# A scan's product for four channel groups in one instruction, the experts' second product by halves, and a new order of the work, in a six-layer transformer and state-space kernel

## The chip, the cores and the metric

The kernel runs on one core of a Trainium2 chip. The metric is the device time in microseconds (us). The core has five engines that run side by side, each with its own queue of instructions: TensorE (PE in the profile; PEld is its loading of weights), VectorE (DVE), ScalarE (ACT), GpSimd (POOL) and SyncE (SP), which issues nearly all transfers here. An engine takes its instructions strictly in the order of its queue, so one that waits holds up all behind it. SBUF is the on-chip memory of 128 partitions; PSUM holds TensorE's results, in 8 banks of 128x512 float32.

## The reference

Four rows of 512 tokens with 128 features go through six residual layers, each on a layer norm of `x`:

```python
x = x + 0.5 * tree(ln(x))      # T: three routed trees give q, k, v; then one attention
x = x + attention(ln(x))       # h: 16 heads, rope, slopes
x = x + 0.5 * tree(ln(x))      # t
x = x + 0.5 * experts(ln(x))   # e: 8 experts, top 2, and a shared one
x = x + mamba(ln(x))           # s: state-space scan
x = x + 0.5 * experts(ln(x))   # f
```

An expert is `(silu(x @ w1.T) * (x @ w3.T)) @ w2.T`, here computed for all 8 and weighted with the routing weight (zero for those not taken), and a ninth, shared expert without a weight. The state-space layer has 256 channels with 16 states each:

```python
def step(h, inp):
    x_t, dt_t, B_t, C_t = inp
    dA = jnp.exp(dt_t[..., None] * A)
    h = dA * h + (dt_t * x_t)[..., None] * B_t[:, None, :]
    y = jnp.einsum('bdn,bn->bd', h, C_t)
    return (h, y)
```

## The kernel before

**Layout.** Features or channels lie on partitions and the 512 tokens of a row along the free axis. Each of the four rows is a chain of its own through the six layers, and layers of different rows run side by side. The names T0 to T3, h0 to h3, t0, e0, s0, f0 and so on are layer and row. A row's layer can start when the same row's layer before it is done.

**The scan (`state_main`).** A tile of 128 partitions holds 32 channels times 4 states. For each half `c` of the channels (2) there are four channel groups `g` of 32 and four state groups `q` of 4, so 32 tiles of 128x512 in each row, 128 in all. For one of them: TensorE spreads B over the partitions into PSUM (`state_b`, once for each `q`, L976); ScalarE makes the decay, `exp(dt * A)`, into a PSUM bank (L988); DVE multiplies `state_b` with `dtxs` (dt times x, L989) and runs the scan over the tokens in place (L990); GpSimd multiplies with C (`cs`, L991). When the four groups of a `q` are through, TensorE adds up their states (`sums`, L941). `dts` and `dtxs` come by transfers that read a row of channels from DRAM four times over (`spread`), 256 KB each: one of each for every `g`, eight for a half.

**The experts (`expert_main`).** For expert `e` and half `c`, TensorE makes two first products of three matmuls each in a rounded float32 format (helper `mm3`, L173 to L175; a number is split into a high and a low part), ScalarE a tanh (L765), DVE two products (L766, L772; in one case of nine GpSimd does the second one). This gives `u0` and `u1`. `second` multiplies both with `w2` into one PSUM bank: 8 matmuls of 128x128 in float32, 4 token tiles `i` times 2 halves `c`, which run as 16 passes (L780). For the 8 routed experts ScalarE scales the result (L790) and GpSimd adds it to `x` (L791); for the shared one, the last, DVE scales and adds in one (L793). When the last layer of a row is done, `store` writes it in one transfer of 256 KB (L1013).

**What sets the order.** Three things. `TIMES` gives each layer of each row a start and an end in arbitrary units for its preparation and its main part; the steps of all jobs are recorded in the order of these times. Inside a job, later steps are put off by a count of steps (`LAG` for trees, `LAG_MIX` for attention, `LAG_EXPERT`, `LAG_STATE`), so that, for instance, `sums` of a `q` are recorded five scan steps after its last group. The framework's own scheduler then moves instructions of one engine past each other and assigns addresses; the numbers in `BUFS` limit how many buffers of a kind are in use at once, and `BANKS` the same for PSUM. So a change of times or buffers changes the order on every engine, that of the transfers in SyncE's queue too.

Of the kernel before, what the change touches and what calls it, by code (L numbers as in the profile page):

```python
# [21 lines left out]
ALU = mybir.AluOpType  # L22
AX = mybir.AxisListType

P = 128
# [13 lines left out]


TIMES = dict(
    loads=(-189.8, -159.8),
    split=(19.6, 79.6),
    T0=(-58.8, -46.7, -14.1, 23.0, 12.7, 34.3),
    T1=(-1.4, 10.7, 26.1, 58.8, 60.4, 75.2),
    T2=(117.2, 127.5, 80.3, 138.4, 137.5, 160.7),
    T3=(97.6, 109.7, 125.5, 214.9, 203.8, 239.4),
    h0=(18.3, 35.0, 46.6, 115.7),
    h1=(85.2, 102.6, 114.5, 205.2),
    h2=(176.0, 193.3, 208.5, 282.9),  # L50
    h3=(241.0, 257.7, 278.8, 374.3),
    t0=(194.1, 204.5, 200.8, 246.1, 245.5, 261.8),
    t1=(326.8, 331.0, 355.5, 422.5, 467.1, 493.7),
    t2=(389.1, 402.4, 396.2, 454.3, 452.2, 490.1),
    t3=(466.1, 478.2, 486.9, 527.6, 531.1, 552.6),
    e0=(283.2, 284.2, 274.8, 345.6),
    e1=(397.8, 412.1, 420.6, 483.0),
    e2=(493.7, 507.9, 514.9, 572.4),
    e3=(570.5, 584.7, 588.8, 639.0),
    consts=(473.4, 474.4),  # L60
    s0=(360.4, 403.4, 402.0, 488.0),
    s1=(470.9, 515.1, 513.4, 595.5),
    s2=(570.4, 613.4, 617.5, 703.4),
    s3=(638.4, 681.3, 690.0, 776.9),
    f0=(572.6, 586.8, 621.9, 690.9),
    f1=(645.2, 659.4, 665.3, 729.5),
    f2=(702.6, 716.8, 728.6, 797.0),
    f3=(798.5, 810.1, 787.3, 878.5),
)
HEAD_LAG = 0.39  # L70

# [34 lines left out]

# [6 lines left out]
def macaron(ctx: ExitStack, tc: tile.TileContext, t: dict, stages: int = 6):  # L113
# [641 lines left out]
    def expert_main(b, st, last):  # L755
        xn = st.xn
        weights = [fetch_expert(e) for e in range(AHEAD)]

        def first(e, c):
            w13 = [weights[e][0][:, k, :] for k in range(2)]  # L760
            ps1, ps3 = bank("moe_1"), bank("moe_3")
            mm3(ps1, [m[:, ts(c, P)] for m in w13], xn)
            mm3(ps3, [m[:, ts(2 + c, P)] for m in w13], xn)
            u = work(f"u{c}")
            nc.scalar.activation(u, ps1, AF.Tanh, scale=0.5)  # L765
            nc.vector.scalar_tensor_tensor(u, u, 1.0, ps1, ALU.add, ALU.mult)  # L766
            if (2 * e + c) % POOL_E[0] < POOL_E[1]:
                v = work("v3")
                nc.scalar.copy(v, ps3)
                nc.gpsimd.tensor_mul(u, u, v)  # L770
            else:
                nc.vector.tensor_mul(u, u, ps3)  # L772
            return u

        def second(e, h):
            w2 = weights[e - e % 4][1]
            acc = bank("moe_acc")
            for i in range(NT):
                for c in range(2):
                    nc.tensor.matmul(  # L780
                        acc[:, ts(i, P)],
                        lhsT=h[c][:, ts(i, P)],
                        rhs=w2[:, e % 4 * 2 + c, :],
                        start=(c == 0),
                        stop=(c == 1),
                    )
            if e < EXPERTS:
                y = work("y")
                for i in range(NT):
                    nc.scalar.mul(y[:, ts(i, P)], acc[:, ts(i, P)], st.comb[:, i, e : e + 1])  # L790
                nc.gpsimd.tensor_add(flat(x[b]), flat(x[b]), y)  # L791
            else:
                nc.vector.scalar_tensor_tensor(  # L793
                    flat(x[b]), acc, 0.25, flat(x[b]), ALU.mult, ALU.add
                )
# [136 lines left out]
    def state_main(b, st, consts):  # L932
# [4 lines left out]
        def sums(c, q, hs, last):  # L937
            if q == 0:
                accs[c] = bank("state_acc")
            for g in range(4):  # L940
                mm = nc.tensor.matmul(  # L941
                    accs[c][32 * g : 32 * g + 32, :],
                    lhsT=gather,
                    rhs=hs[g],
                    start=(q == 0),
                    stop=(q == GROUPS - 1),
                )
# [16 lines left out]

        later = Later(LAG_STATE)
        for c in range(2):
            dt, dtx = [], []
            rows = t["state_rows"][b, c].rearrange("m (g r) s -> m g r s", r=CH)
            for g in range(4):
                for m, (name, to) in enumerate((("dts", dt), ("dtxs", dtx))):  # L970
                    to.append(work(name))
                    spread(to[g], rows[m, g])
            for q in range(GROUPS):

                bs = bank("state_b")
# [4 lines left out]
                    start=True,  # L980
                    stop=True,
                )
                hs = []
                for g in range(4):
                    k = (4 * c + g) * GROUPS + q
                    dA, h = bank("decay"), work("states")
                    hs.append(h)
                    nc.scalar.activation(dA, dt[g], AF.Exp, scale=A[:, k : k + 1])  # L988
                    nc.vector.tensor_mul(h, bs, dtx[g])  # L989
                    nc.vector.tensor_tensor_scan(h, dA, h, 0.0, ALU.mult, ALU.add)  # L990
                    last = nc.gpsimd.tensor_mul(h, h, cs[:, q])  # L991
                    later.step()
                    yield
# [356 lines left out]
```

## Time and profile before

| What | Value |
|---|---|
| time, median of 3 runs (lowest, highest) | 1130.23 us (1128.74, 1132.4) |
| the profiled execution's own time | 1134.71 us |
| its span, first to last instruction | 1132.9 us |
| granted clock of TensorE, mean | 0.983 |
| TensorE busy from 0 to 28 us | 10.96 us |
| TensorE, DVE busy from 300 to 600 us | 299.10, 223.88 us |
| TensorE, DVE busy from 600 to 1050 us | 409.47, 422.95 us |
| last matmuls of the layers s0, s1, s2, s3 | 683, 827, 988, 1074 us |
| first matmul of f3's experts | 1083 us |

In the profile's groups stand line, engine and operation, the tiles written and read with shape, the number of instructions, then the busy time in us and the mean duration of one in ns, then the idle time of the engine just before them and what ended it. In a table of windows the columns are, after the stretch and its length, busy time and number of instructions of PE, PEld, DVE, ACT and POOL, then the clock granted to TensorE (1.00 is full speed), the share of time that the transfer engines were busy, and GB/s. In a timeline: start, length, engine, line, operation, tiles and count; in brackets the idle time before it and what ended that.

### The profile page before, as it was taken

To read this page: it belongs to the slowest core of one execution; us is meant where nothing else is said; L and a number is where in the kernel's file an instruction comes from. 1 tells how busy PE (TensorE), PEld (TensorE's weight loads), DVE (VectorE), ACT (ScalarE), POOL (GpSimd) and SP (SyncE) were. 2 spreads that over 40 slices of the span, in tenths; PEclk is the share of its full clock that TensorE was granted. 3 is DMA by queue.
4 is the path that set the end of the run, shared out by engine and by line. 5 is a ranking of instruction groups with operands and counts; after the bars stand their busy time and mean duration, and the time that the engine had idled before them with its cause. 6 is when DMAs were issued, how large, how long until landed. Compare 5 with 4: busy or idle time off the path is not lost.

```text
span 1132.9 us, 16461 instructions
## 1 busy us (share of the span) xinstructions
PE 1065.0 (94%) x5536; PEld 717.4 (63%) x5536; DVE 903.5 (80%) x2151; ACT 516.4 (46%) x1078; POOL 408.3 (36%) x392
## 2 busy tenths in 40 slices
PE   3999999999999999999999999999598989997998
PEld 2666655566666767765566766567276646754787
DVE  4566886587576887775799997899989989999864
ACT  2231423332322555444443544465576557564544
POOL 2215231002100323220324651356626647666523
PEclk9999999999999999999999999999899989997999
DMA  7885845321542212243743334832137424742320
GB/s 217 261 254 168 284 109 119 84 69 57 123 124 93 65 37 69 87 112 115 208 137 139 117 94 107 277 130 107 38 117 254 133 66 146 249 121 70 113 88 10
DMA packets 79651, 146.41 MB, mean 129 GB/s; under 512 B 7536, under 2 KB 39664, under 8 KB 79568
## 3 DMA queue, kind: packets, MB, share of 16 engines
q1 hardware_dynamic: 79280, 145.07, 42.6%
q8 instruction: 44, 0.72, 0.3%
q14 instruction: 39, 0.32, 0.1%
q10 hardware_dynamic: 288, 0.30, 0.1%
HBM read 125.35 MB, written 13.70 MB: 123 GB/s over the span
## 4 chain that ended last, share of the span: by engine, by line
PE 61%; DVE 17%; issue 4%; ACT 4%; POOL 2%; DMA 1%; SPq 1%; POOLq 0%; ACTq 0%; DVEq 0%
PE tree_acc L410 9%; PE moe_acc L780 7%; DVE states L990 6%; PE head_acc L608 4%; PE head_sc L640 4%; PE moe L173 4%; PE head_max L564 4%; PE moe L175 3%; PE moe L174 3%; DVE states L989 3%; PE tree_mm L173 3%; PE tree_mm L175 3%; PE tree_mm L174 3%; PE state_acc L941 2%; DVE u L766 2%
## 5 line engine op out<-in xcount | busy, mean ns | idle before, releaser
L991 POOL TENSOR_TENSOR states<-states,cs 128x512 f32<-128x512 f32 x128 | 163.8, 1284 | 146.0 <-DVE states L990 87.8
L410 PE MATMUL tree_acc<-full,ring 128*128 128x512 f32 x384 | 193.4, 599 | 5.9 <-DVE full L400 4.9
L572 DVE CUSTOM_DVE_ANT_0 head_max<-head_max,kept 128x128 f32<-128x128 f32 (+3 forms) x256 | 126.8, 495 | 61.0 <-PE head_max L564 58.5
L400 DVE SCALAR_TENSOR_TENSOR full<-tree_mm,kept,mask 128x512 f32<-128x512 f32 x188 | 137.8, 746 | 42.4 <-PE tree_mm L175 37.7
L656 ACT ACTIVATE pt<-head_sc 128x512 f32<-128x512 f32 (+1 forms) x176 | 95.3, 559 | 139.2 <-PE head_sc L648 132.4
L780 PEld LDWEIGHTS moe_acc<-ring,u 128*128 128x128 f32 x1152 | 141.9, 195 | 21.2 <-DVE u L772 6.2
L990 DVE TENSOR_TENSOR_SCAN states<-decay,states 128x512 f32<-128x512 f32 x128 | 154.8, 1216 | 0.5 <-ACT decay L988 0.2
L780 PE MATMUL moe_acc<-ring,u 128*128 128x128 f32 x1152 | 146.4, 280 | 5.3 <-DVE u L772 3.1
L173 PE MATMUL moe<-xl,ring 128*128 128x512 f32 x288 | 129.1, 448 | 13.3 <-DVE u L766 4.7
L791 POOL TENSOR_TENSOR kept<-kept,y 128x512 f32<-128x512 f32 x64 | 83.0, 1298 | 142.2 <-ACT y L790 133.7
L988 ACT ACTIVATE decay<-dts,kept 128x512 f32<-128x512 f32 x128 | 88.5, 696 | 83.9 <-DVE states L990 67.0
L765 ACT ACTIVATE u<-moe 128x512 f32<-128x512 f32 x144 | 86.4, 601 | 72.2 <-PE moe L175 70.5
L174 PE MATMUL moe<-xh,ring 128*128 128x512 f32 x288 | 116.8, 405 | 0.0
L175 PE MATMUL moe<-xh,ring 128*128 128x512 f32 x288 | 115.7, 402 | 0.0
L766 DVE SCALAR_TENSOR_TENSOR u<-u,moe 128x512 f32<-128x512 f32 x144 | 97.4, 678 | 17.7 <-ACT u L765 15.2
L790 ACT ACTIVATE y<-moe_acc,scratch 128x128 f32<-128x128 f32 x256 | 73.3, 367 | 74.5 <-PE moe_acc L780 72.6
L548 POOL TENSOR_SCALAR km<-k_bias,kept 128x512 fp32r<-128x512 f32 x64 | 43.6, 699 | 157.2 <-PE head_sc L640 110.6
L173 PE MATMUL tree_mm<-xl,ring 128*128 128x512 f32 x188 | 98.1, 524 | 0.2 <-DVE states L990 0.2
L173 PEld LDWEIGHTS moe<-xl,ring 128*128 128x128 f32 x288 | 55.1, 191 | 63.5 <-DVE u L766 13.5
L410 PEld LDWEIGHTS tree_acc<-full,ring 128*128 128x128 f32 x384 | 70.8, 191 | 38.4 <-issue 19.9
L564 PE MATMUL head_max<-km,q_bias 120*128 120x512 f32 (+2 forms) x192 | 92.0, 479 | 1.1 <-ACT p L446 1.1
L989 DVE TENSOR_TENSOR states<-state_b,dtxs 128x512 f32<-128x512 f32 x128 | 85.9, 683 | 4.7 <-DMA dtxs<-state_rows 3.6
(257 smaller groups left out, 1946.1 us busy)
## 6 DMA issues: line engine op xcount, KB each, us to landing
ring<-moe_parts SPq DMA_DIRECT2D x72, 512.0 KB
ring<-tree_parts SPq DMA_DIRECT2D x42, 512.0 KB
ring<-in_fff_w SPq DMA_DIRECT2D x24, 512.0 KB
mask<-fff_taken SPq DMA_DIRECT2D x48, 256.0 KB
ring<-in_moe_w SPq DMA_DIRECT2D x16, 512.0 KB
dts<-state_rows SPq DMA_DIRECT2D x32, 256.0 KB
dtxs<-state_rows SPq DMA_DIRECT2D x32, 256.0 KB
moe_parts<-moe_w SPq DMA_DIRECT2D x9, 512.0 KB
```

The costliest lines, as they stand in the source:

```text
L173: nc.tensor.matmul(ps, lhsT=lh, rhs=rl, start=start, stop=False)
L174: nc.tensor.matmul(ps, lhsT=ll, rhs=rh, start=False, stop=False)
L175: nc.tensor.matmul(ps, lhsT=lh, rhs=rh, start=False, stop=stop)
L400: nc.vector.scalar_tensor_tensor(full, ps, neg_b1[:, n : n + 1], st.masks[k][:, c, :], ALU.max, ALU.mult)
L410: nc.tensor.matmul(acc, lhsT=weights[k][1][:, c, :], rhs=h, start=(c == 0), stop=False)
L564: nc.tensor.matmul(view, lhsT=qs[:R_MAX, g, ts(i, P)], rhs=km[j0 // 2][:R_MAX, j0 % 2 : j0 % 2 + each, :kw], start=True, stop=True,)
L572: nc.vector.tensor_tensor_reduce(view[:, n, :], view[:, n, :], future[:, S - kw :], -1.0, float(np.finfo(np.float32).max), ALU.add, ALU.mi ...
L766: nc.vector.scalar_tensor_tensor(u, u, 1.0, ps1, ALU.add, ALU.mult)
L780: nc.tensor.matmul(acc[:, ts(i, P)], lhsT=h[c][:, ts(i, P)], rhs=w2[:, e % 4 * 2 + c, :], start=(c == 0), stop=(c == 1),)
L989: nc.vector.tensor_mul(h, bs, dtx[g])
L990: nc.vector.tensor_tensor_scan(h, dA, h, 0.0, ALU.mult, ALU.add)
L991: last = nc.gpsimd.tensor_mul(h, h, cs[:, q])
```

## The change

It has five parts.

1. In the scan, one DVE product of 128x2048 takes the place of four of 128x512. `state_b` is read four times over. `states` becomes one tile for the four groups of a `q`, and `dtxs` one tile for the four groups of a half, filled by four transfers as before. The scans, GpSimd's products and the sums work on slices.
2. The experts' second product runs over the halves `c` outside and the token tiles `i` inside; only the first matmul of the bank starts it and only the last one closes it.
3. For the shared expert of the last layer of row 3, the order is by token tiles as before, DVE adds each 128x128 tile by itself, and each is stored at once by a transfer of 64 KB. The other rows are stored as before.
4. `TIMES` has new values for nearly all jobs, and LAG goes from 5 to 6, LAG_MIX from 4 to 3, LAG_STATE from 5 to 6.
5. The buffer counts change: `xl`, `v3`, `dt`, `pos` and `dts` have one fewer, `u1` and `xs` one more, `dtxs` goes from 6 tiles of 128x512 to 2 of 128x2048, and `states` from 8 of 128x512 to 8 of 128x2048. In the built programs the new `states` lie at three addresses and `dtxs` at two.

In the built programs the transfers of one half's `dts` and `dtxs`, which alternated, now go out with the four of `dtxs` together. At the start, the first tree's second weights (`fff_w2_0`) stand behind three of the small attention weights instead of one.

```diff
@@ TIMES (some of them)
-    loads=(-189.8, -159.8),
+    loads=(-149.2, -119.2),
-    T2=(117.2, 127.5, 80.3, 138.4, 137.5, 160.7),
+    T2=(94.5, 104.8, 73.9, 132.0, 128.3, 151.5),
-    h2=(176.0, 193.3, 208.5, 282.9),
-    h3=(241.0, 257.7, 278.8, 374.3),
+    h2=(171.0, 188.3, 208.5, 309.7),
+    h3=(247.4, 264.1, 297.6, 393.1),
...
-    f2=(702.6, 716.8, 728.6, 797.0),
-    f3=(798.5, 810.1, 787.3, 878.5),
+    f2=(684.0, 698.2, 722.7, 791.1),
+    f3=(845.7, 859.1, 830.7, 935.8),
@@
-LAG, LAG_MIX, LAG_EXPERT, LAG_STATE = 5, 4, 3, 5
+LAG, LAG_MIX, LAG_EXPERT, LAG_STATE = 6, 3, 3, 6
@@ BUFS (what changes of each line)
-    **dict(ring=7, stage=5, b1=1, b2=1, ln=3, xh=1, xl=4),
+    **dict(ring=7, stage=5, b1=1, b2=1, ln=3, xh=1, xl=3),
-    **dict(moe_w=1, lgT=1, u0=4, u1=2, y=2, v3=2),
-    **dict(hid=1, xs=2, sz=2, conv=1, xd=1, xb=2, cs=1, dt=2, dtx=2, pos=2, dts=7, dtxs=6, states=8),
+    **dict(moe_w=1, lgT=1, u0=4, u1=3, y=2, v3=1),
+    **dict(hid=1, xs=3, sz=2, conv=1, xd=1, xb=2, cs=1, dt=1, dtx=2, pos=1, dts=6, dtxs=2, states=8),
@@ expert_main, second
-            for i in range(NT):
-                for c in range(2):
-                    nc.tensor.matmul(
-                        acc[:, ts(i, P)],
-                        lhsT=h[c][:, ts(i, P)],
-                        rhs=w2[:, e % 4 * 2 + c, :],
-                        start=(c == 0),
-                        stop=(c == 1),
-                    )
+            at_end = last and b == B - 1 and e == EXPERTS
+            order = [(c, i) for c in range(2) for i in range(NT)]
+            for c, i in sorted(order, key=lambda ci: ci[::-1]) if at_end else order:
+                nc.tensor.matmul(
+                    acc[:, ts(i, P)],
+                    lhsT=h[c][:, ts(i, P)],
+                    rhs=w2[:, e % 4 * 2 + c, :],
+                    start=(c == 0 and (at_end or i == 0)),
+                    stop=(c == 1 and (at_end or i == NT - 1)),
+                )
...
-            else:
+            elif not at_end:
                 nc.vector.scalar_tensor_tensor(
                     flat(x[b]), acc, 0.25, flat(x[b]), ALU.mult, ALU.add
                 )
+            else:
+                for i in range(NT):
+                    out = x[b][:, i, :]
+                    nc.vector.scalar_tensor_tensor(out, acc[:, ts(i, P)], 0.25, out, ALU.mult, ALU.add)
+                    nc.sync.dma_start(out=t["out"][b, ts(i, P)], in_=out)
...
-        if last:
+        if last and b < B - 1:
             store(b)
@@ state_main
-                    rhs=hs[g],
+                    rhs=hs[:, g, :],
...
-            dt, dtx = [], []
+            dt, dtx = [], work("dtxs", (4, S))
             rows = t["state_rows"][b, c].rearrange("m (g r) s -> m g r s", r=CH)
             for g in range(4):
-                for m, (name, to) in enumerate((("dts", dt), ("dtxs", dtx))):
-                    to.append(work(name))
-                    spread(to[g], rows[m, g])
+                dt.append(work("dts"))
+                for m, to in enumerate((dt[g], dtx[:, g, :])):
+                    spread(to, rows[m, g])
...
-                hs = []
+                hs = work("states", (4, S))
+                nc.vector.tensor_mul(hs, dtx, bs.unsqueeze(1).to_broadcast([P, 4, S]))
                 for g in range(4):
                     k = (4 * c + g) * GROUPS + q
-                    dA, h = bank("decay"), work("states")
-                    hs.append(h)
+                    dA, h = bank("decay"), hs[:, g, :]
                     nc.scalar.activation(dA, dt[g], AF.Exp, scale=A[:, k : k + 1])
-                    nc.vector.tensor_mul(h, bs, dtx[g])
                     nc.vector.tensor_tensor_scan(h, dA, h, 0.0, ALU.mult, ALU.add)
```

More of the change, by code (lines that the diff above doesn't have):

```diff
@@ L41 @@
 TIMES = dict(
-    loads=(-189.8, -159.8),
-    split=(19.6, 79.6),
-    T0=(-58.8, -46.7, -14.1, 23.0, 12.7, 34.3),
+    loads=(-149.2, -119.2),
+    split=(20.2, 80.2),
+    T0=(-58.9, -46.8, -14.2, 22.9, 11.2, 32.8),
     T1=(-1.4, 10.7, 26.1, 58.8, 60.4, 75.2),
-    T2=(117.2, 127.5, 80.3, 138.4, 137.5, 160.7),
-    T3=(97.6, 109.7, 125.5, 214.9, 203.8, 239.4),
-    h0=(18.3, 35.0, 46.6, 115.7),
-    h1=(85.2, 102.6, 114.5, 205.2),
-    h2=(176.0, 193.3, 208.5, 282.9),
-    h3=(241.0, 257.7, 278.8, 374.3),
[L52 to L58, printed above, removed]
+    T2=(94.5, 104.8, 73.9, 132.0, 128.3, 151.5),
+    T3=(97.6, 109.7, 125.5, 214.9, 202.7, 238.3),
+    h0=(16.2, 32.9, 44.5, 113.6),
+    h1=(88.3, 105.7, 119.2, 209.5),
+    h2=(171.0, 188.3, 208.5, 309.7),
+    h3=(247.4, 264.1, 297.6, 393.1),
+    t0=(180.6, 191.0, 207.3, 252.6, 252.0, 268.3),
+    t1=(341.1, 345.3, 355.5, 416.0, 447.6, 471.6),
+    t2=(393.5, 406.8, 392.6, 450.7, 446.3, 484.2),
+    t3=(467.1, 479.2, 487.9, 528.6, 532.1, 553.6),
+    e0=(283.3, 284.3, 274.7, 345.5),
+    e1=(397.1, 411.4, 420.6, 482.5),
+    e2=(488.0, 502.2, 511.0, 583.7),
     e3=(570.5, 584.7, 588.8, 639.0),
[L60 to L63, printed above, removed]
+    consts=(529.0, 530.0),
+    s0=(360.3, 403.2, 401.9, 483.8),
+    s1=(470.9, 515.2, 513.4, 599.3),
+    s2=(560.1, 603.1, 617.5, 703.4),
     s3=(638.4, 681.3, 690.0, 776.9),
-    f0=(572.6, 586.8, 621.9, 690.9),
+    f0=(570.9, 585.1, 621.8, 690.8),
     f1=(645.2, 659.4, 665.3, 729.5),
-    f2=(702.6, 716.8, 728.6, 797.0),
-    f3=(798.5, 810.1, 787.3, 878.5),
+    f2=(684.0, 698.2, 722.7, 791.1),
+    f3=(845.7, 859.1, 830.7, 935.8),
 )
```

## The prediction

> **What bounds the kernel now.** I read the page's busy lines first, then the table of windows, the groups of VectorE by form, TensorE's waits, and last the timelines around the scan.
>
> ```profile
> PE 1065.0 (94%) x5536; PEld 717.4 (63%) x5536; DVE 903.5 (80%) x2151; ACT 516.4 (46%) x1078; POOL 408.3 (36%) x392
> 300.00:600.00 300.00, 299.10 (x1658) 195.20 (x1657) 223.88 (x650) 135.94 (x278) 62.25 (x71) 1.00 0.38 109
> 600.00:1050.00 450.00, 409.47 (x2070) 278.20 (x2068) 422.95 (x783) 248.26 (x515) 242.64 (x196) 0.96 0.41 133
> 1050.00:1133.00 83.00, 76.77 (x477) 64.34 (x471) 53.50 (x102) 38.95 (x100) 31.83 (x25) 1.00 0.22 72
> ```
>
> The 94% of TensorE is a mean over two regimes. From 300 to 600 us it is busy for 299.1 of 300 us: nothing that VectorE (DVE) gains there is worth anything. From 600 to 1050, where rows 0 to 3 scan while experts run beside them, DVE is busy for 423 of 450 us (94%) and TensorE for 409, at a granted clock of 0.96: there DVE sets the pace. The last 50 us hold row 3's last experts alone and are TensorE's again.
>
> ```profile
> L990 DVE TENSOR_TENSOR_SCAN states<-decay,states 128x512 f32<-128x512 f32 x128 | 154.8, 1216 | 0.5 <-ACT decay L988 0.2
> L989 DVE TENSOR_TENSOR states<-state_b,dtxs 128x512 f32<-128x512 f32 x128 | 85.9, 683 | 4.7 <-DMA dtxs<-state_rows 3.6 <-PE state_b L976 0.7 <-PE state_acc L941 0.2
> L572 DVE CUSTOM_DVE_ANT_0 head_max<-head_max,kept 128x512 f32<-128x512 f32 x64 | 44.6, 696 | 25.3 <-PE head_max L564 25.1
> L572 DVE CUSTOM_DVE_ANT_0 head_max<-head_max,kept 128x128 f32<-128x128 f32 x64 | 18.9, 295 | 9.1 <-PE head_max L564 8.3
> 798.93 1.28 DVE L989 TENSOR_TENSOR states<-state_b,dtxs 128x512 f32<-128x512 f32 x2
> 800.11 2.34 DVE L990 TENSOR_TENSOR_SCAN states<-decay,states 128x512 f32<-128x512 f32 x2
> ```
>
> The product to be grouped is L989; L572 shows what DVE's time is made of. Two products end to end take 1.28 us, not 2 x 0.683: an instruction's last 83 ns lie under the next one.
>
> ```profile
> PE state_acc L941 <- POOL states L991: 13.7, 10, 7.4
> PE moe L173 <- DVE u L766: 4.7, 5, 1.9
> PE moe L173 <- DVE states L990: 3.8, 7, 0.8
> PE moe_acc L780 <- DVE u L772: 3.1, 6, 0.7
> ```
>
> TensorE's waits of the second half: sums behind the scan, and experts behind DVE.
>
> ```profile
> 721.33 1.20 SPq L930 DMA_DIRECT2D dtxs<-state_rows  x2
> 724.76 0.69 DVE L989 TENSOR_TENSOR states<-state_b,dtxs 128x512 f32<-128x512 f32 x1 [2.42 <-DMA dtxs<-state_rows]
> 860.01 0.69 DVE L989 TENSOR_TENSOR states<-state_b,dtxs 128x512 f32<-128x512 f32 x1 [1.22 <-DMA dtxs<-state_rows]
> 1127.70 1.26 POOL L791 TENSOR_TENSOR kept<-kept,y 128x512 f32<-128x512 f32 x1 [1.89 <-ACT y L790]
> 1128.99 0.69 DVE L793 SCALAR_TENSOR_TENSOR kept<-moe_acc,kept 128x512 f32<-128x512 f32 x1 [2.60 <-POOL kept L791]
> 1129.71 0.39 SPq L1013 DMA_DIRECT2D out<-kept  x1
> ```
>
> In rows 1 and 2 the very first product waits for its transfer, and DVE with it. The last three lines are the kernel's end.
>
> **1. One product for four groups: -5.6 us.** 128 products become 32 of 128x2048. L572 gives the price of an element: (696 - 295) / 384 = 1.044 ns. A 512 product issues in 1.28 - 0.683 = 0.60 us, of which 512 x 1.044 = 0.535 is elements and 0.065 is the instruction. Three of these go per group: 32 x 3 x 0.065 = 6.3 us of DVE. The difference of plain durations (4 x 683 - (683 + 1536 x 1.044) = 445 ns, 14.3 us in all) counts the overlapped 83 ns as well; I don't take it, but it bounds the gain. The other end is 0: the trace has no product of 2048 elements with a repeated PSUM operand, and if that form paid for each 512 anew, nothing would be saved. 112 of the 128 products lie between 600 and 1050, so 28 of the 32 groups count: 28 x 0.20 = 5.6. The four earlier ones lie under TensorE. A grouped product holds DVE for 2.2 us instead of 0.6, so an experts' u behind it comes up to 1.6 us later; in exchange three of the four scans stand without a product ahead of them. Inside a DVE-bound stretch that evens out.
>
> **2. The four dtxs in one tile: +1 us (-4 to +11).** The first product of a half now waits for four transfers instead of one. In row 1 the built order issued two dts, then the first dtxs at 721.33; it landed by 724.76. Now it is two dts and four dtxs, so the awaited one stands three places later: three issues of 0.62 us (1.9 us), or, if the engines set the rate, three times 256 KB at the page's best 283 GB/s (2.8 us). Queued behind a waiting product are the scans and the u of the experts, and then TensorE. But the order also puts more DVE work ahead of it: between the last steps of the state preparation (from L913) and the first product stand 11.4, 11.1, 12.0 and 28.8 us of DVE work in rows 0 to 3 before, and 13.9, 12.6, 17.9 and 27.8 after (sums of each instruction's mean share of DVE's time, in the two orders as built). Row 1: +2.8 - 1.5 = +1.3 on top of its 2.4; row 2: the extra 5.9 swallows 2.8 and the old 1.2: -1.2; row 0 has its slack; row 3 waited for state_b, not for the transfer, and its transfers stood from 956 to 970 for a product at 975.5: up to +1. Together about +1. Ends: -4 (both old waits gone, 3.6) and +11 (2.8 in each of four rows, none covered).
>
> **3. The experts' second product by halves: -1 us (-3 to 0).** The 8 matmuls and their 16 passes stay. With c outside, 8 passes of 112 ns (1.78 us / 16) run before u1 is needed. Only the part of the 3.1 us of waits ahead of L780 that is for u1 can go; the matmuls that waited longest read u0 in five of six cases. Queued behind are the next expert's first products.
>
> **4. Row 3's end by tiles: 0 us (-0.3 to +0.6).** All four adds still wait for one POOL addition (1127.70 to 1128.96). DVE then needs 3 x 0.26 + 0.35 = 1.13 us (L468, 128x128: 345 ns long, 261 start to start) instead of 0.69. The last store is issued about 0.7 us later than 1129.71 and moves a quarter: the 256 KB's packets ran for 1.03 us (1130.63 to 1131.66), a quarter of which is 0.26. So +0.7 - 0.77. The Trainium skill speaks against it: "DMA: Bandwidth & Descriptors", rules for kernel authors, has transfers under 64 KB as mostly overhead and wants them coalesced, with a fixed share of about 2.0 us in each. By that rule the last quarter would land no sooner after its issue than the whole does, and the end would cost about +0.7; the trace's 2.3 us from issue to semaphore with 1.03 us of packets in it is why I take 0.
>
> **5. The new order: -3 us (-11 to +10).** Only sums over the two built orders tell something here. (a) TensorE goes from float32 to rounded float32 428 times before, 412 after; the first rounded matmul then takes 314 ns instead of 231 where the trace shows it: 16 x 0.083 = -1.3, counted half, as half of it lies under DVE: -0.7. (b) Up to row 1's first experts, the TensorE-bound stretch, stand 572.6 us of TensorE work before and 568.3 after, with equal DVE work (406.3). From there to f3: TensorE 445.1 before, 449.5 after; DVE 460.7 and 453.8 (part 1 is in that). So 4.3 us of matmuls move under the DVE-bound stretch. If they hide entirely, -4.3; if they are paid there, 0. That stretch took 506 us for 461 of DVE work, so it is not one engine's alone; half: -2.2. (c) Junctions, where a row changes from scan to experts, are as in the old order: from e2's last u to e3's first u stand 26 us of DVE work before, 24 after. The bounds are those of the waits a new order could remove or make: the half-clock stretches below on one side, as much again on the other.
>
> The startup keeps its chain (normalization, routing, masks at 26.4 us). The first w2 is now issued behind two more small loads, but it has from 5 to 27 us: 0. Fewer buffers for dt, pos, xl and v3 free long before their next row: 0, and part of (c)'s bounds if not. LAG values act only through the order.
>
> Sum: -5.6 + 1 - 1 + 0 - 2.9 = -8.5. The profiled execution took 1134.7 us (span 1132.9), 4.5 above the median of 1130.2; it would come to 1126.2. Against the median: 1130.2 - 8.5 = 1121.7; I say 1122.
>
> A second weighing, on the clock. The granted clock fell to half in five stretches after 800 us, the longest 802 to 812, around the idle 7.4 us of L941, and 1024 to 1034. The Trainium skill ("TensorE: Matmul & The Clock Gate", part 1) has the gate close after an idle window of about 3.4 us; the trace agrees at 802 (idle 7.4) but at 1024 no single gap was longer than 1.9 us. By the rule only the first stretch could go with shorter waits, by the rows all five. The sum leaves both out.
>
> **The rivals.**
> A, slower: the tile of four transfers. All eight halves wait, not four, and 2.8 us each: 22 us against the 9.5 of gains, 1130.2 + 12.9 = 1143. It decides from 1.2 us per half on. For it: L989 already waits on DMA, DVE is in order. Against: the second halves are loaded far ahead, and row 2 has 5.9 us more cover.
> B, no difference: the gain of DVE goes into waits on TensorE or ScalarE, or the big product is no cheaper. Then parts 3 and 5a remain, -1.7: 1128.5. For it: 506 us for 461 of DVE work.
> C, much faster: the half-clock stretches and the waits of L941 (13.7) shrink with the shorter DVE queue. In the 34.1 us at half clock TensorE is busy for 26.2 and so loses 13.1: 1130.2 - 8.5 - 13.1 = 1109.
>
> **How the numbers follow.** A difference under 0.3% (3.4 us) can't be told from none. Forecast (1115 to 1126.8): 0.42. C: 0.14. B (1126.8 to 1133.6): 0.16. A and junctions worse than before: 0.28. So faster 0.56, same 0.16, slower 0.28. The range leaves out about 1 in 10 at each end: below 1107 (C and more) and above 1143 (A). The forecast's own range is 1115 to 1127.
>
> **What would show it.** Right: 32 products of about 2.28 us, DVE's total 6 us lower, TensorE's idle time from 600 to 1050 (40 us) smaller. Part 2 wrong: waits of the first products for DMA above 2.5 us in more than one row. Part 4 wrong: over 4 us from the last POOL addition to the end. Part 5 wrong: TensorE gaps above 3 us at junctions other than s1's end.

## The result, and the profile after

The changed kernel takes 1134.16 us (median of 10 executions, 1132.01 to 1138.08), the kernel before beside it 1130.56 (10 executions, 1128.0 to 1132.4). The ratio is 1.0028, 95% interval 1.0017 to 1.0040: 0.3% slower, where 1122 us and a gain were forecast. The value lies in the range, on the wrong side.

The profiled execution after has a time of its own of 1134.84 us and a span of 1133.0, 0.7 above its median. The one before (1134.71, span 1132.9) lay 4.2 above its median, so the two traces show equal spans for kernels whose medians are 3.6 us apart. A second profile of the kernel before (run e11, own time 1132.05, span 1130.3) serves where that matters.

The page's busy line and the table of windows of the kernel after, with the columns as before:

```profile
PE 1062.6 (94%) x5536; PEld 714.4 (63%) x5536; DVE 896.0 (79%) x2058; ACT 518.5 (46%) x1078; POOL 407.8 (36%) x392
300.00:600.00 300.00, 297.02 (x1609) 192.71 (x1610) 220.38 (x631) 135.10 (x277) 65.01 (x73) 1.00 0.37 107
600.00:1050.00 450.00, 408.33 (x2139) 279.69 (x2139) 418.98 (x705) 251.20 (x517) 238.88 (x194) 0.98 0.43 136
1050.00:1133.00 83.00, 75.13 (x450) 61.45 (x448) 53.78 (x102) 38.20 (x98) 32.20 (x26) 0.98 0.18 58
```

VectorE (DVE) works 7.5 us less than before, where 6.3 were forecast. But TensorE's idle time from 600 to 1050 us, which should have shrunk, went from 40.5 to 41.7 us.

VectorE's groups by form, after:

```profile
L997 DVE TENSOR_TENSOR_SCAN states<-decay,states 128x512 f32<-128x512 f32 x128 | 153.8, 1209 | 0.3
L992 DVE TENSOR_TENSOR states<-dtxs,state_b 128x2048 f32<-128x2048 f32 x32 | 72.9, 2279 | 1.8 <-DMA dtxs<-state_rows 0.9 <-PE state_b L984 0.8
```

One product of 2048 takes 2.279 us; 2.28 was worked out. Its waits for a transfer are 0.9 us in all, where they had been 3.6.

TensorE's waits behind 600 us, after (total, times, longest):

```profile
PE state L324 <- POOL hid L318: 7.5, 1, 7.5
PE moe L173 <- DVE states L997: 6.1, 12, 1.3
PE moe L173 <- DVE u L766: 5.2, 7, 1.2
PE moe_acc L783 <- DVE u L766: 4.8, 4, 1.8
PE state_acc L949 <- POOL states L998: 4.7, 6, 1.5
PE moe L173 <- DVE u L772: 2.6, 4, 1.1
PE moe_acc L783 <- DVE u L772: 2.4, 3, 1.5
```

The scan's sums wait for 4.7 us instead of 13.7. The single wait of 7.4 us has not gone, though. Before, the sums of row 1's scan wait from 800 to 808 us; after, the preparation of row 2's (`hid`) waits from 803 to 811 us. It is nearly the same place, and in both traces VectorE works there without a break; another instruction stands first in TensorE's queue. The experts' waits for VectorE shown here grew from 11.6 to 21.1 us.

Where VectorE's saving went shows in windows: the first 500 us, the rest, and of the rest the 100 us up to the border at 600 that the prediction used and what lies behind it. First the kernel before, then after:

```profile
0.00:500.00 500.00, 479.44 (x2530) 314.40 (x2532) 349.96 (x1107) 180.31 (x378) 110.94 (x150) 1.00 0.47 131
500.00:1133.00 633.00, 585.54 (x3011) 403.00 (x3010) 553.50 (x1045) 336.10 (x700) 297.33 (x242) 0.97 0.40 128
500.00:600.00 100.00, 99.30 (x471) 60.47 (x471) 77.05 (x161) 48.90 (x87) 22.85 (x22) 1.00 0.49 152
600.00:1133.00 533.00, 486.24 (x2541) 342.54 (x2539) 476.45 (x885) 287.21 (x613) 274.48 (x221) 0.97 0.38 123
```

```profile
0.00:500.00 500.00, 481.51 (x2507) 314.78 (x2508) 343.09 (x1082) 181.30 (x378) 114.33 (x155) 1.00 0.46 130
500.00:1133.00 633.00, 581.12 (x3031) 399.62 (x3029) 552.87 (x977) 337.24 (x700) 293.45 (x237) 0.98 0.41 129
500.00:600.00 100.00, 97.65 (x449) 58.47 (x450) 80.11 (x172) 47.84 (x86) 22.37 (x19) 1.00 0.50 152
600.00:1133.00 533.00, 483.47 (x2586) 341.15 (x2585) 472.76 (x806) 289.40 (x615) 271.08 (x219) 0.98 0.39 124
```

In the first 500 us, where TensorE sets the pace and VectorE has 150 us to spare, VectorE now does 6.9 us less. Behind 500 us it works 552.9 us instead of 553.5 (552.6 in e11). The scans were made cheaper, but the new order has moved nearly as much of VectorE's work (the largest piece by layer is 3.4 us of row 3's attention) from the stretch where it is free to a later one. Part of that landed between 500 and 600 us, where VectorE works 3.1 us more and TensorE, busy nearly without a break before, stands idle for 2.4 us instead of 0.7. Behind 600 us VectorE works 3.7 us less (2.8 less than in e11), so about half of the saving is left there.

The end of the kernel after:

```profile
1126.91 1.26 POOL L794 TENSOR_TENSOR kept<-kept,y 128x512 f32<-128x512 f32 x1 [1.88 <-ACT y L793]
1128.21 0.89 DVE L802 SCALAR_TENSOR_TENSOR kept<-moe_acc,kept 128x128 f32<-128x128 f32 x4 [2.60 <-POOL kept L794]
1128.53 2.06 SPq L803 DMA_DIRECT2D out<-kept  x4
```

From the end of GpSimd's last addition (1128.17) to the end of the span stand 4.84 us, against 3.96 before. The four additions take 0.89 us, less than reckoned; the four issues take 2.06 us, so that SyncE's issues, not the additions, set when the last store leaves.

### The profile page after: what moved, and what is told of

The parts are those of the page before. It is cut to its first block, busy times and chain, and to the rows that moved or that the text cites. A ratio compares the mean times of both kernels' runs of the same rounds, so it can differ in the third digit from the quotient of the medians.

```text
span 1133.0 us, 16290 instructions
## 1 busy us (share of the span) xinstructions
PE 1062.6 (94%) x5536; PEld 714.4 (63%) x5536; DVE 896.0 (79%) x2058; ACT 518.5 (46%) x1078; POOL 407.8 (36%) x392
## 4 chain that ended last, share of the span: by engine, by line
PE 67%; DVE 21%; issue 5%; DMA 2%; POOL 2%; ACT 2%; SPq 1%; POOLq 0%; DVEq 0%; ACTq 0%
PE tree_acc L410 13%; PE moe_acc L783 7%; DVE states L997 6%; PE head_acc L608 5%; DVE states L992 4%; PE tree_mm L173 4%; PE head_max L564 4%; PE moe L173 4%; PE head_sc L640 4%; PE moe L174 3%; PE tree_mm L174 3%; PE moe L175 3%; PE tree_mm L175 3%; DVE u L766 3%; DVE u L772 2%
## 5 line engine op out<-in xcount | busy, mean ns | idle before, releaser
L766 DVE SCALAR_TENSOR_TENSOR u<-u,moe 128x512 f32<-128x512 f32 x144 | 96.7, 675 | 27.1 <-ACT u L765 26.6
L175 PE MATMUL moe<-xh,ring 128*128 128x512 f32 x288 | 114.9, 399 | 0.0
L174 PE MATMUL moe<-xh,ring 128*128 128x512 f32 x288 | 114.7, 398 | 0.0
L173 PE MATMUL tree_mm<-xl,ring 128*128 128x512 f32 x188 | 92.8, 496 | 2.2 <-DVE pT L453 1.3
L772 DVE TENSOR_TENSOR u<-u,moe 128x512 f32<-128x512 f32 x128 | 86.0, 675 | 2.5 <-PE moe L175 0.4
```

What stands on the lines that cost most here:

```text
L173: nc.tensor.matmul(ps, lhsT=lh, rhs=rl, start=start, stop=False)
L174: nc.tensor.matmul(ps, lhsT=ll, rhs=rh, start=False, stop=False)
L175: nc.tensor.matmul(ps, lhsT=lh, rhs=rh, start=False, stop=stop)
```

## The experiments

Theory at the start (T1): the new product is a gain and some other part of the change eats it. Rival (T2): the grouped product is itself the loss, as it holds VectorE for 2.28 us. From the second series on a third theory led: each order fits one code, and an order that doesn't fit costs more than any part of this change is worth. (In the expectations this is theory S, and T2 is theory P.) `TIMES`, `LAG` and `BUFS` were only ever changed together, so what one of them costs is open.

### The two orders and the two codes crossed, and two parts alone

e1: the code of after with `TIMES`, `LAG` and `BUFS` of before. e2: the code of before with those of after (with enough buffers for tiles that stand alone).

```
e1  -TIMES, LAG, BUFS of after     +those of before, dtxs=2
e2  -TIMES, LAG, BUFS of before    +those of after, dtxs=8, states=12
```

> The changed code (parts 1 to 3) with the times, lags and buffer counts of before (dtxs 2 of the large tiles). If the new order is what costs: the code's gain of some 6 us shows, 1122 to 1127 us. If the grouped product or its tiles give nothing or cost: 1130 to 1137 us. DVE's busy time should be 6 to 7 us under before's 903.5 either way.

> The code of before with the new times, lags and buffer counts (dtxs 8 and states 12 of the small tiles). If the new order costs by itself: 1134 us or more, at DVE's old busy time of 903. If the order is worth what I took for it (-3 us) and the code is what costs: 1126 to 1130 us.

e3: the grouped product with its tiles alone, in the order of before. e4: the experts' second product by halves alone.

```
e3  -                hs = []
    +                hs = work("states", (4, S))
    +                nc.vector.tensor_mul(hs, dtx, bs.unsqueeze(1).to_broadcast([P, 4, S]))
    ...
    -                    nc.vector.tensor_mul(h, bs, dtx[g])
e4  -            for i in range(NT):
    -                for c in range(2):
    +            for c in range(2):
    +                for i in range(NT):
```

> Part 1 alone (grouped product, its tiles) with the times and lags of before. By the price of an instruction, 0.065 us x 96: DVE busy 897 and, if DVE's time in the second half is the span's, 1124 to 1126 us. If the gain goes into DVE's idle time instead: 1129 to 1132 us at the same busy time. If the one tile of four transfers holds DVE up: over 1133 us, with waits for dtxs well above before's 3.6 us.

> Part 2 alone: the experts' second product by halves, all else as before; on ScalarE, GpSimd and SyncE the order is unchanged. Forecast -1 us: 1129 to 1130.5. If halves are worth nothing: 1130.5 within 0.2%. If the sums' order costs TensorE something (the accumulation of a token tile is spread over the bank): over 1133.

| run | median us | ratio to before (95%) | DVE busy | PE busy |
|---|---|---|---|---|
| e1: code after, order before | 1148.29 | 1.0152 (1.0130 to 1.0175) | 901.6 | 1073.2 |
| e2: code before, order after | 1144.86 | 1.0116 (1.0095 to 1.0136) | 899.4 | 1070.1 |
| e3: product alone, order before | 1148.03 | 1.0147 (1.0126 to 1.0169) | 900.8 | 1069.3 |
| e4: halves alone | 1129.80 | 0.9990 (0.9976 to 1.0005) | 902.4 | 1061.1 |

Either code loses 13 to 17 us in the other's order, and e3 alone loses as much as e1. The times of e1 and the first two ranges for e3 were missed, and VectorE's total fell by 2 to 3 us in them, not by 6. That looks like T2. But e3's group of products speaks against a stall at the product as the main cause:

```profile
L984 DVE TENSOR_TENSOR states<-dtxs,state_b 128x2048 f32<-128x2048 f32 x32 | 73.0, 2281 | 10.2 <-PE tree_tr L324 4.8 <-PE state_b L976 4.5 <-PE state_acc L941 0.8
```

Its price is 2.281 us, and no transfer is among its main waits. The idle time ahead of it rose from 4.7 to 10.2 us, by waits for TensorE, which is a third of the loss at most. On the other hand the framework's scheduler moved 160 of 4354 instructions on TensorE, 246 of 1050 on ScalarE and 59 of 466 in SyncE's queue when only the product's form was changed. (These counts compare the two orders as built, line numbers aside.) Halves alone move 14 instructions on TensorE and lie within the measurement of no change, from -2.7 to +0.6 us.

### Four products in the new tiles, and the order alone

e6 and e8 have the tiles of four slices but four products; e6 in the order of after, e8 in that of before. e9 and e10 change no instruction of the kernel before: each number in `TIMES` is moved at random by at most 0.6.

```
e6, e8  -                nc.vector.tensor_mul(hs, dtx, bs.unsqueeze(1).to_broadcast([P, 4, S]))
        +                    nc.vector.tensor_mul(h, bs, dtx[:, g, :])
e9      -    h3=(241.0, 257.7, 278.8, 374.3),
        +    h3=(241.4, 257.8, 279.0, 373.9),
        ...
```

> The kernel after, its order and its tiles of four slices, but with four products of 128x512 into the slices in place of one of 128x2048. Theory S (every piece of code needs an order fitted to it; the product itself is a small gain): VectorE's total rises by 6 to 14 us, and the time by more than that, since the order was found for the big product: 1142 to 1150 us. Theory P (the big product itself costs time, because it holds VectorE for 2.28 us and waits for its bank in VectorE's queue, and the order only wins part of that back): VectorE's total rises alike, but the time falls, to 1122 to 1131 us.

> The kernel before with dtxs and states in one tile of four slices each, but still four products of 128x512, in the times of before. The scheduler then moves 190 of 2153 instructions on VectorE, 60 of 1050 on ScalarE, 49 of 466 on SyncE's queue. Theory S: some 5 to 15 us lost, since the order no longer fits: 1136 to 1147 us. Theory P: the tiles cost nothing by themselves, the product did: 1128 to 1134 us, and the whole 16 us of the grouped product alone belong to the instruction.

> The kernel before, with every start and end in its table of times moved at random by at most 0.6 units (some 0.6 us); no instruction is changed, 474 of 4354 on TensorE, 436 of 2153 on VectorE and 123 of 1050 on ScalarE stand elsewhere in their queues. Theory S: 1138 to 1150 us, as much as the grouped product lost in the old order. Theory P: within 4 us of the kernel before, 1128 to 1135 us.

> As the run with the times moved at random by at most 0.6 units, with other random numbers: 516 of 4354 instructions on TensorE, 566 of 2153 on VectorE, 96 of 1050 on ScalarE stand elsewhere. Theory S: 1138 to 1150 us. Theory P: 1128 to 1135 us. Two of them tell how far two such orders lie apart.

| run | median us | ratio to before (95%) | DVE busy | PE busy |
|---|---|---|---|---|
| e6: four products, order after | 1143.49 | 1.0101 (1.0084 to 1.0119) | 903.8 | 1070.8 |
| e8: four products, tiles, order before | 1140.77 | 1.0080 (1.0061 to 1.0100) | 905.8 | 1064.6 |
| e9: order of before, shifted | 1146.19 | 1.0126 (1.0105 to 1.0147) | 905.2 | 1075.3 |
| e10: order of before, shifted otherwise | 1153.46 | 1.0190 (1.0169 to 1.0212) | 905.8 | 1076.2 |

T2 is not needed to explain e3: shifts that change nothing but the order cost 14 and 21 us, as much as e3 lost. An experiment that moves hundreds of instructions measures the fit of the order first. What the order does is visible on TensorE, whose busy time rises by 10 us in e9 and e10 with the same 5536 matmuls. Part of it can be named. Attention's weighting of the values takes four heads one by one; a head's weights are 128 x 32 (`128*32` in the lines), so its result fills 32 of the 128 rows, and each of its matmuls in float32 is two passes. This group in before, e10 and after:

```profile
L608 PE MATMUL head_acc<-pt,vv 128*32 128x512 f32 (+3 forms) x512 | 56.8, 444 | 0.1
```

```profile
L608 PE MATMUL head_acc<-pt,vv 128*32 128x512 f32 (+3 forms) x512 | 65.5, 444 | 0.0
```

```profile
L608 PE MATMUL head_acc<-pt,vv 128*32 128x256 f32 (+3 forms) x512 | 60.1, 444 | 0.0
```

The same 512 passes of the same mean duration cover 56.8, 65.5 and 60.1 us, since they lie over each other to a different degree. TensorE's timeline shows why: first the kernel before, then e10, at the same place of row 2:

```profile
442.81 0.23 PE L648 MATMUL head_sc<-kept 128*128 128x128 bf16 x1
442.97 1.07 PE L608 MATMUL head_acc<-pt,vv 128*32 128x512 f32 x8
443.97 0.50 PE L564 MATMUL head_max<-km,q_bias 120*128 120x512 f32 x1
```

```profile
451.41 1.05 PE L608 MATMUL head_acc<-pt,vv 128*32 128x512 f32 x2
452.39 0.39 PE L564 MATMUL head_max<-km,q_bias 120*128 120x256 f32 x1
452.71 1.06 PE L608 MATMUL head_acc<-pt,vv 128*32 128x512 f32 x6
```

Eight passes for four heads, unbroken, hold TensorE for 1.00 us until the next matmul. Broken off after one head, the two take 0.98 us and the other six 0.99. In an unbroken run the passes go side by side: the first passes of the four heads start 7 ns apart, and the second ones some 450 ns behind them. A matmul with 128 columns of weights between them ends that, and the rest pays the whole duration again. (The Trainium skill, "TensorE: Matmul & The Clock Gate", part 3, has 32-column tiles of the array work concurrently; 8 passes in 1.00 us beside 2 in 0.98 agree.) The passes stand in 70 unbroken runs before, 76 in after, 83 in e10. With the time counted from each pass to the next matmul, attention's weighting takes 52.1, 56.3 and 61.1 us (1.3 and 1.2 us of the last two are idle time behind a run). It lies almost wholly in the stretch that TensorE bounds, and by the first matmul of row 1's second trees e10 is 12.5 us behind; attention's weighting took 50.9 us up to there instead of 42.3, two thirds of that.

This is not the whole of what an order costs. Counted alike, attention's weighting takes 57.6 us in e9, but only 53.4 to 53.8 in e1, e2, e3 and e6, so 2 us at most of their losses of 11 to 17; the rest was not traced to a place. And the order of after gains elsewhere on TensorE: the scan's sums, matmuls on 32 rows too, cover 46.0 us instead of 52.8 (51.1 in e11), and TensorE's total is that of e11, 1062.6.

### The end alone, the kernel before again, and the heads kept together

e5: row 3's end by tiles alone; here no other instruction moves on any engine. e11: the kernel before, unchanged. e12: the kernel after, in which the four heads' matmuls are told to the scheduler as beginning together, as the scan's sums are. e13: e12 with the old end.

```
e12  +                if j < 3:
     +                    tc.add_manual_dep(getattr(mm, "ins", mm), last.name, ...
     +                        reason="mixes of four heads begin together")
e13  -            at_end = last and b == B - 1 and e == EXPERTS
     +            at_end = False
     -        if last and b < B - 1:
     +        if last:
```

> The kernel before with part 4 alone: row 3's last product by tiles, each tile added and stored by itself; no instruction elsewhere is moved. The prediction had 0 (-0.3 to +0.6). The trace after showed 4.84 us from the last addition of GpSimd to the end, against 3.96 before; if that is the edit's doing, this run is 0.9 us above the kernel before, with the stores' issues on SyncE 0.45 to 0.8 us apart; if it is chance, the difference is within 0.3 us.

> The kernel before once more, for a second profile, since the first one's own time lay 4.2 us above the median. Theory: the first profile's surplus lies in half-clock stretches (34.1 us of them after 800 us) and will be 3 to 5 us smaller here; the work of TensorE in runs of 32-row matmuls (attention 52.1 us in 70 runs) is the same to 0.3 us. Rival: the surplus is spread evenly and the half-clock stretches are as long.

> The kernel after, with the four 32-row matmuls of attention's weighting of the values (four heads) made to begin together, as the sums of the scan already do: their runs on TensorE fall from 76 to 71, and 96 of 4354 instructions on TensorE stand elsewhere. Theory W (TensorE's busy time depends on how often runs of 32-row matmuls are broken off, since within a run one follows 85 ns after the other and the last holds 523 ns): 5 x 0.44 = 2.2 us less, 1132 us. Rival (any moved order loses 10 us or more): 1140 to 1150 us.

> As the run with the four heads together, with row 3's end as it was before (by halves, one addition, one store). If the end by tiles costs 0.9 us, 1131 us, level with the kernel before; if not, as the run with the heads together alone.

| run | median us | ratio to before (95%) | DVE busy | PE busy |
|---|---|---|---|---|
| e5: end by tiles alone | 1132.72 | 1.0025 (1.0014 to 1.0036) | 902.6 | 1062.5 |
| e11: before again | 1131.03 | 1.0011 (0.9999 to 1.0022) | 902.5 | 1062.6 |
| e12: after, heads together | 1133.02 | 1.0022 (1.0006 to 1.0037) | 895.5 | 1055.9 |
| e13: e12 with the old end | 1130.18 | 1.0003 (0.9994 to 1.0012) | 895.2 | 1056.7 |

e11 is the yardstick: the same kernel differs from itself by 1.3 us in this series, so single differences under some 1.5 us are not told apart. Its half-clock stretches behind 800 us are 27.2 us instead of 34.1, a larger difference than the 3 to 5 expected, and attention's weighting is again 52.1 us in 70 runs.

The end by tiles costs time, but its size is only bounded. The timelines' last lines in e11 and e5:

```profile
1125.04 1.26 POOL L791 TENSOR_TENSOR kept<-kept,y 128x512 f32<-128x512 f32 x1 [1.88 <-ACT y L790]
...
1127.05 0.39 SPq L1013 DMA_DIRECT2D out<-kept  x1
```

```profile
1125.30 1.26 POOL L794 TENSOR_TENSOR kept<-kept,y 128x512 f32<-128x512 f32 x1 [1.88 <-ACT y L793]
1126.60 0.88 DVE L802 SCALAR_TENSOR_TENSOR kept<-moe_acc,kept 128x128 f32<-128x128 f32 x4 [2.60 <-POOL kept L794]
1126.92 1.76 SPq L803 DMA_DIRECT2D out<-kept  x4
```

From GpSimd's last addition to the end stand 4.0 us in e11 (1126.30 to 1130.3) and 4.34 in e5 (1126.56 to 1130.9): 0.3 us in these traces, 0.9 in that of after; e12 and e13, whose orders on TensorE are the same, have 4.7 and 3.9, which is 0.8. The medians put e5 1.7 us above e11 and 3.0 above the rest of the series. At an equal granted clock of 0.986 five executions of e5 have a mean of 1132.6 and five of the kernel before 1131.2, which is 1.4. The medians put e12 2.8 us above e13. So the end by tiles costs between 0.3 and 3 us.

In e12 the heads' runs fall from 76 to 71 and their group's busy time from 60.1 to 56.9 us, which is more than the 2.2 us expected. (That trace is of an execution of 1129.02 us, 4.0 below the median; the expectation's 85 ns from one pass to the next is a mean over steps of 7 and of some 450 ns.)

```profile
L608 PE MATMUL head_acc<-pt,vv 128*32 128x256 f32 (+3 forms) x512 | 56.9, 444 | 0.0
```

The expected 1132 is within its spread (1128.73 to 1137.79), but 1133.02 by itself can't be told from after. With the old end besides, e13 is level with the kernel before. So the two named losses, together 3.2 + 0.9 = 4.1 us by the traces, are of the size of the difference of 3.6 between after and before, and taking both away brings the kernel level. The split between them is not shown: by the medians the heads are worth 1.1 us (1134.16 to 1133.02, in different series) and the end 2.8, and 96 matmuls also stand elsewhere in e12 and e13. Neither explains why the gain that was forecast is missing as well. No version beat the kernel before beyond the measurement's uncertainty.

### One product against four, the order shifted alike

Left open was what the grouped product is worth by itself. Three pairs have the new order with the same random shift (at most 0.6) of t3, e1 to e3, s0 to s3 and f0 to f3, one with one product, one with four.

```
     -    s1=(470.9, 515.2, 513.4, 599.3),
     +    s1=(470.9, 514.7, 513.0, 599.0),
     ...
four -                nc.vector.tensor_mul(hs, dtx, bs.unsqueeze(1).to_broadcast([P, 4, S]))
     +                    nc.vector.tensor_mul(h, bs, dtx[:, g, :])
```

In the second and third pair the shift prepares row 0's last experts ahead of row 3's first; the routing factors' two places in scratch then take turns the other way, and some of row 0's last routed experts are scaled by row 1's factors. These four kernels therefore give a different output and serve for their times alone; number and size of all instructions stay.

> The kernel after with the times of the scans, of the experts beside them and of t3 moved at random by at most 0.6 units (first random numbers). If after's order is fitted as before's was, 1139 to 1150 us; if not, 1131 to 1137 us. With its partner of four products: the one product is 5.6 us faster by part 1's term, 0 by the theory that the order decides.

> The same shifted times (first random numbers) with four products of 128x512 into slices of the same tile. Part 1's term: 5.6 us above its partner of one product (0 to 14.3). The theory that the order decides: within 8 us of it, with either sign.

> The kernel after with the second half's times moved by second random numbers of at most 0.6 units. If after's order is fitted, 1139 to 1150 us; if not, 1131 to 1137 us. With its partner: 5.6 us faster by part 1's term, either sign by the theory that the order decides.

> The same shifted times (second random numbers) with four products of 128x512. Part 1's term: 5.6 us above its partner of one product (0 to 14.3). The theory that the order decides: within 8 us of it, with either sign.

> The kernel after with the second half's times moved by third random numbers of at most 0.6 units. If after's order is fitted, 1139 to 1150 us; if not, 1131 to 1137 us. With its partner: 5.6 us faster by part 1's term, either sign by the theory that the order decides.

> The same shifted times (third random numbers) with four products of 128x512. Part 1's term: 5.6 us above its partner of one product (0 to 14.3). The theory that the order decides: within 8 us of it, with either sign.

| shift | one product: us, ratio (95%) | four products: us, ratio (95%) | difference us |
|---|---|---|---|
| first | 1140.94, 1.0084 (1.0052 to 1.0116) | 1148.74, 1.0157 (1.0124 to 1.0190) | 7.8 |
| second | 1144.96, 1.0121 (1.0090 to 1.0151) | 1150.66, 1.0161 (1.0123 to 1.0200) | 5.7 |
| third | 1146.75, 1.0147 (1.0119 to 1.0175) | 1147.76, 1.0150 (1.0126 to 1.0174) | 1.0 |

One product is faster in all three, by 4.8 us in the mean, near part 1's 5.6. Three pairs with this spread (standard error 2.0) don't exclude zero. Unshifted, after and e6 lie 8.3 us apart the same way (1.0101 - 1.0028); in the old order e3 and e8 lie 7.3 apart the other way. Both members of a pair also differ in where the scheduler put some 170 to 180 of TensorE's instructions, so this is evidence for the product's worth in the new order, and no proof of its size. The shifts alone cost the kernel after 7 to 13 us. All five random shifts, two of before and three of after, made the kernel slower; that both orders are fitted to their codes is the likely reason, though nothing here tells how the orders were found. Few moved instructions need not cost anything: e4 with 14 and e12 with 96 on TensorE lost nothing.

## Why the prediction was wrong, step by step

**What bounds the kernel.** Right in kind: VectorE's stretch behind 600 us is where a saving counts. It was read as a fixed amount of work there, and that amount was free to change with the order. The border at 600 us was a round number: what VectorE has to do just ahead of it also counts.

**Part 1, -5.6.** The price was right (2.279 us measured, 2.28 worked out), and VectorE's total fell by 7.5 us, of which 6.3 were reckoned. The pairs give -4.8, not excluding 0. The groups lie where "28 of the 32 groups count" has them, but the gain did not stay there: VectorE's work fell by 3.7 us behind 600 us and by 0.6 behind 500, since the order brought other work in.

**Part 2, +1 (-4 to +11).** The waits for the tile of four transfers did not come; the product's waits for transfers fell from 3.6 to 0.9 us, so that the term had the wrong sign. Rival A is excluded as the cause.

**Part 3, -1 (-3 to 0).** Alone: -2.7 to +0.6. Consistent, not resolved.

**Part 4, 0 (-0.3 to +0.6).** Wrong. It was 0.9 in the trace of after, 0.3 in that of e5, 0.8 between those of e12 and e13, and 1.4 by the means at one clock. The term "3 x 0.26 + 0.35 = 1.13 us" for VectorE was too high (0.89), but behind it the one issue per store was left out: four issues take 1.76 to 2.06 us on SyncE, and the last is queued behind three. The falsifier set for it, over 4 us from the last addition to the end, was met (4.84). The rule weighed there (the Trainium skill, "DMA: Bandwidth & Descriptors", rules for kernel authors: transfers under 64 KB are mostly overhead) stood for +0.7, nearer than the 0 that was taken. But these stores have just 64 KB, the page's 2.0 us is a fit to transfers issued by GpSimd, and what the trace shows is the issues on SyncE.

**Part 5, -3 (-11 to +10).** This is the step that failed and decided the sign: the new order was put at -2.9 us and cost about +8, by subtraction (below). (a) counted how often TensorE changes its number format, worth 1.3 us by the prediction's own price; the runs of 32-row matmuls, worth more, were not looked at (attention's weighting, mostly before 600 us: 70 to 76 runs, 52.1 to 56.3 us). (b) took 4.3 us for work moved under VectorE's stretch: up to row 1's first experts the trace shows 592.7 before and 592.1 after, 0.6. The same comparison of built orders did say that VectorE had equal work up to that point (406.3 in each), with part 1 hardly begun there; that the first 500 us had become lighter and the end heavier was not looked up at a second cut. (c) "junctions as in the old order": TensorE's long wait stands at the same junction as before, only ahead of another instruction, so the sign that the prediction had named (a gap above 3 us at another junction) did not appear: behind 811 us no gap is longer than 1.8 us. Of the 8 us some pieces can be named: 3.3 us more of busy time in attention's weighting (60.1 against 56.8) and 1.7 us more of idle TensorE between 500 and 600 us, against 5 to 7 us gained in the scan's sums. Where the rest lies stays open.

**The sum and the chances.** By subtraction the order is worth about +8 us here: 3.6 measured, less -4.8 (product), -1.2 (halves) and +1.2 (end, between the trace's 0.9 and 1.4). The pairs' -4.8 is uncertain, so the 8 is too; with a product worth nothing, it would be 3.6. That is within the bounds given for it, but the forecast put a gain into the middle. The sum treated the parts as independent and the order as a small term. The runs show the order moving the time by 7 to 21 us where the times were shifted or a product's form or tiles changed without a new order, about as much as all other terms together or more. That the value lay in the stated range is owed to the width that rivals A and B gave it.

**The second weighing.** Half-clock stretches behind 800 us fell from 34.1 us (27.2 in e11) to 23.9 with the change, a small gain at most, and rival C did not happen. At 802 us the trace agrees with the rule on the idle window less well than was said: TensorE fell idle at 800.4 us and the clock at 801.9, after 1.5 us. Rival B, the gain going into waits on ScalarE and TensorE, may be part of the truth: VectorE's waits for ScalarE before the experts' u rose from 15.2 to 26.6 us, 6.8 of it behind 500 us (12.3 to 19.1).

## What to carry to other kernels

Where a scheduler's order has been searched for one code, price an edit in two steps, the instruction and the re-ordering it brings, and size the second by shifting the schedule at random without any edit; here that alone cost 14 to 21 us beside a saving of 6. Cut the built orders at the border between the stretches that two engines bound, at more than one place, and compare each engine's work on both sides: other work that the order moves in can use up a saving. Matmuls on 32 rows are cheap only in unbroken runs (here some 0.6 us for each run more: 70, 76 and 83 runs, 56.8, 60.1 and 65.5 us busy), so count the runs and tell the scheduler which of them belong together.

## What the runs showed of the hardware

- Four heads' 32-row matmuls of 512 columns take 1.00 us as one run of eight passes and 0.98 + 0.99 us if a matmul with 128 columns of weights stands between the first head and the rest. For 384, 256 and 128 columns a run of two takes 0.76, 0.55 and 0.34 us, one of eight 0.78, 0.57 and 0.36. All are counted from the first pass to the next matmul.
- The time of one and the same kernel goes with the granted clock, roughly: of 33 executions of the kernel before in one series the twelve at a clock of 0.991 have a mean of 1128.6 us, the thirteen at 0.989 one of 1129.8, the three at 0.985 one of 1131.6 (the three at 0.988 too). One half-clock stretch of 3.4 us is 0.0015 of the mean clock. The Trainium skill ("TensorE: Matmul & The Clock Gate", part 1) has the clock fall after an idle window of about 3.4 us; the trace of after has such a stretch at an idle time of 7.5 us, but the clock falls at 805.0 us, 1.9 us after the last matmul, and the half-clock stretches at 921, 952 and 1085 us come although no gap behind 811 us is longer than 1.8 us.
- Four stores of 64 KB issued one behind the other hold SyncE for 1.76 to 2.06 us, one of 256 KB for 0.39.
